# Short last chunks, small last groups and denominators by Ln and Exp in a two-part graph network kernel

## The chip, the core and the metric

The kernel runs on one core of a Trainium2 chip. Its time is the device time of one execution in microseconds (us); the time before is the median of 3 runs. The engines of the core work side by side, each through its own queue in order: PE (TensorE, matrix multiplies), DVE (VectorE), ACT (ScalarE), POOL (GpSimd, here nothing but indirect DMAs) and SP (the queue that issues the plain DMAs). They meet at semaphores.

## The reference

A graph of 10000 nodes with 64 features, and 160000 edges, sorted by their target dst. Part 0 has four layers (L = 4) of this convolution, between layer norms and residual sums:

```python
def _genconv(x, src, dst, ea, W1, b1, lg, lb, W2, b2, t):
    m = jax.nn.relu(x[src] + ea) + EPS
    logits = m * t
    mx = jax.ops.segment_max(logits, dst, num_segments=N)
    e = jnp.exp(logits - mx[dst])
    denom = jax.ops.segment_sum(e, dst, num_segments=N)
    alpha = e / denom[dst]
    agg = jax.ops.segment_sum(m * alpha, dst, num_segments=N)
    h = agg + x
    h = h @ W1 + b1
    h = jax.nn.relu(_ln(h, lg, lb))
    return h @ W2 + b2
```

Part 1 is one attention layer: K and V of the source node, Q of the target node and a projected edge feature give a score per head, `exp(clip(score, -5, 5))`; the output is the sum of V times score over the edges of a node, added to x.

## The kernel before, in words

**Stages.** An encoder over the nodes; index preparation; then for each layer l = 0 to 3 a loop over the edges (`softmax_layer(l)`) and a loop over the nodes (`node_layer(l)`); then a last edge loop (`attention_layer`), and a closing loop over the nodes that adds the residual and stores the output. After node layer 0, `clear_queries` sets the buffer `qs` in DRAM to zero with 157 DMAs on SP's queue; the scheduler puts 36 of them into the prologue and 121 between the stores of softmax layer 0 and the table rows of node layer 0.

**Edge loops.** The edges are worked from both ends at once: the first half forwards in partitions 0 to 63, the second half backwards in 64 to 127. There are NG = 625 groups of 128 edges for each half, taken in chunks of CG = 4 groups, so NC = 157 chunks: 156 of 512 columns and a last one of 128. For every group POOL issues two gathers (L603) of 128 rows of the node table, one for each half: 1250 for each edge loop. `front` adds them on PE to the transformed edge features (L687, L689), ACT makes the logits (L692, L693), and a scan on DVE (L699) gives the running maximum. `decay` writes the factor exp(-rise) into the PSUM tile `dec`, which has one buffer; `back` runs one chunk behind, with the product me (L727), the scans se (denominator, L729) and sm (numerator, L732), two transposes (L758), and four stores to the DRAM buffer st0 (L762). With the last chunk the node in the middle, which has edges in both halves, is corrected (L738 to L753). `attention_layer` is built the same way (scores L990 to L1002, back L1008 to L1025) with its store to st1.

**Order.** A scheduler places the instructions of the program on each engine. An object of the class `InOrder`, when called, ties all instructions since its last call, engine by engine, to the order in which the program makes them. It is called once for each chunk in the edge loops, but not after the last `back(NC - 1, *held)`; and once at the end of `node_layer`.

**Node layers.** NT = 79 tiles of 128 nodes, in groups of GRP = 8: ten groups, the last of 7. The stages of a group are spread over several turns i of a software pipeline:

```python
        for i in range(NG2 + (4 if last else 3)):
            at(i - 1, widen)
            at(i, enter)
            at(i - 3, norm_narrow)
            at(i + 1, divide)
            at(i + 2, fetch)
            at(i - 1, spans)
            at(i - 1, norm_wide)
            at(i - 2, narrow)
            if last:
                at(i - 4, project)
            at(i - 3, leave)
```

`fetch` gathers (POOL, L603) each node's numerators and denominators from st0 into n_g (two buffers). `divide` takes the reciprocal on DVE in place (L806) and multiplies into n_h (L807). `enter` transposes in pairs of node tiles and adds the old features (L813, n_hT). `widen` multiplies by W1 into the PSUM tiles pn and ept (L821) and squares on ACT (L825); `spans` averages the squares on PE; `norm_wide` takes Ln and Exp on ACT for the inverse root (n_r, L455 and L456), multiplies on DVE (n_y, L841, which frees pn and ept), and applies gain, bias and relu on ACT (L844). `narrow` multiplies by W2 (L851), adds into XT (L856) and squares (n_sx, L858). `norm_narrow` averages on PE (L863), Ln and Exp on ACT (n_rx), multiplies on DVE (XIT, L872; n_e in the last layer), and relu on ACT (L873). `leave` transposes back and stores the next layer's table rows (n_row L495, SP L487); the next edge loop's first gather needs them all. In the last layer `leave` forms the residual, and `project` makes K, V and Q (n_kvq, one buffer): K and V go to kv_table by SP, Q goes to `qs` by one scatter on POOL for each node tile (L906), each of which waits until the scatter before it has landed. A last scatter (mq, L1063) ends that, and then SP loads q from `qs`.

All tiles of a group are 512 columns wide, also for the last group of 7 tiles; what is missing there is filled by memset.

Of the kernel before, what the change touches and what calls it, by code (L numbers as in the profile page):

```python
# [9 lines left out]
F32 = mybir.dt.float32  # L10
# [3 lines left out]
OP = mybir.AluOpType  # L14
# [12 lines left out]
def kernel(ctx: ExitStack, tc: tile.TileContext, a, out):  # L27
# [21 lines left out]
    NG = HALF // G  # L49
    NC = (NG + CG - 1) // CG  # L50
    W = 1280
# [4 lines left out]
    MX = HALF - MR * MW  # L56
    assert 2 * NG * G == NE and R * W == NE and R <= P and NT <= P and MR < 64 and 0 < MX < MW
    EPS = 1e-7
    LN_EPS = 1e-5
    INV_SQRT_D = float(1.0 / (D // H) ** 0.5)  # L60
    GRP = 8
    groups = [(i, min(GRP, NT - i)) for i in range(0, NT, GRP)]

    const = ctx.enter_context(tc.tile_pool(name="const", bufs=1))
# [7 lines left out]
    def ps_a(shape):  # L72
        return ps("z", shape, 3)
# [377 lines left out]
    PN = GRP // 2  # L451

    def root(t, v):

        nc.scalar.activation(t, v, AF.Ln, bias=lneps)  # L455
        nc.scalar.activation(t, t, AF.Exp, scale=-0.5)  # L456

    def norm_rows(dst, src, n, name):

        mv = work.tile([P, GRP, 2], F32, name=name + "_mv", bufs=2)  # L460
        for i in range(n):
            st = work.tile([P, 6], F32, name=name + "_st", bufs=2)
            nc.vector.bn_stats(st, src[:, i, :])
            nc.vector.bn_aggr(mv[:, i, :], st)
        rs = work.tile([P, GRP], F32, name=name + "_rs", bufs=2)
        root(rs[:, :n], mv[:, :n, 1])
        for i in range(n):
            nc.vector.tensor_scalar(dst[:, i, :], src[:, i, :], mv[:, i, 0:1], rs[:, i:i + 1],
                                    op0=OP.subtract, op1=OP.mult)
        if n < GRP:  # L470
            nc.vector.memset(dst[:, n:, :], 0.0)

    def turn_pairs(rows):

        pt = ps_a([P, PN, P])
        for j in range(PN):
            nc.tensor.transpose(pt[:, j, :], rows[:, 2 * j:2 * j + 2, :].rearrange("p s d -> p (s d)"), ident)
        return pt.rearrange("p j n -> p (j n)")

    def turn_back(cols):  # L480
        pt = ps_a([P, PN, P])
        for j in range(PN):
            nc.tensor.transpose(pt[:, j, :], cols[:, j * P:(j + 1) * P], ident)
        return pt.rearrange("p j (s d) -> p (j s) d", s=2)
# [3 lines left out]

    def of_group(t, i0):
        return t[:, i0 * D:i0 * D + CN]  # L490

# [17 lines left out]
    for i0, n in groups:  # L509
        h = work.tile([P, GRP, D], F32, name="n_h", bufs=2)  # L510
        norm_rows(h, load_x(i0, n), n, "n_a")
        hT = work.tile([P, CN], F32, name="n_hT", bufs=2)
        nc.scalar.activation(hT, turn_pairs(h), AF.Relu)
        pt = ps("oe", [P, CN])
        nc.tensor.matmul(pt, encW, hT, start=True, stop=True)
        nc.scalar.activation(of_group(XIT, i0), pt, AF.Identity, bias=encb)
        to_message_table(tables[0], turn_back(of_group(XIT, i0)), i0, n)

# [87 lines left out]
    def span(k):  # L606
        g0 = k * CG
        n = min(CG, NG - g0)
        return g0, n, slice(g0 * G, (g0 + n) * G)
# [59 lines left out]
    def softmax_layer(l, ea_rows=None):  # L669
# [99 lines left out]
        for k in range(NC):  # L769
# [13 lines left out]
            order()  # L783
        back(NC - 1, *held)

    def node_layer(l):

        last = l + 1 == L
        NG2 = len(groups)
        it = [{} for _ in groups]  # L790
        halves = [slice(s * D, (s + 1) * D) for s in range(2)]
        order = InOrder()

        def fetch(g):
            i0, n = groups[g]
            t = edge.tile([P, GRP, D2], F32, name="n_g", tag="so", bufs=2)
            for i in range(n):
                gather(t[:, i, :], st0, ends[:, i0 + i:i0 + i + 1])
            if n < GRP:
                V.memset(t[:, n:, :], 1.0)  # L800
            it[g]["g"] = t

        def divide(g):
            t = it[g]["g"].rearrange("p n (h i c) -> p n h i c", h=2, i=2)
            h = work.tile([P, GRP, D], F32, name="n_h", bufs=2)
            V.reciprocal(t[:, :, :, 0, :], t[:, :, :, 0, :])  # L806
            V.tensor_mul(h.rearrange("p n (h c) -> p n h c", h=2), t[:, :, :, 1, :], t[:, :, :, 0, :])  # L807
            it[g]["h"] = h

        def enter(g):  # L810
            pt = turn_pairs(it[g]["h"])
            hT = work.tile([P, CN], F32, name="n_hT", bufs=2)
            V.scalar_tensor_tensor(hT, pt, EPS, of_group(XIT, groups[g][0]), op0=OP.add, op1=OP.add)  # L813
            it[g]["hT"] = hT

        def widen(g):
            hT = it[g]["hT"]
            it[g]["w"], it[g]["sq"] = [], []
            for s in range(2):
                pt = ps(("pn", "ept")[s], [P, CN])  # L820
                nc.tensor.matmul(pt, W1[halves[s], l, :], hT[halves[s], :], start=True, stop=True)  # L821
                it[g]["w"].append(pt)
            for s in range(2):
                sq = edge.tile([P, CN], F32, name="n_sq", tag="up")
                S.activation(sq, it[g]["w"][s], AF.Square, bias=b1[:, l:l + 1])  # L825
                it[g]["sq"].append(sq)

        def spans(g):
            it[g]["v"] = []
            for s in range(2):  # L830
                pv = ps(("dec", "hist")[s], [P, CN])
                nc.tensor.matmul(pv, over_all, it[g]["sq"][s], start=True, stop=True)
                it[g]["v"].append(pv)

        def norm_wide(g):
            it[g]["y"] = []
            for s in range(2):
                r = edge.tile([P, CN], F32, name="n_r", tag="e")
                root(r, it[g]["v"][s])
                y = work.tile([P, CN], F32, name="n_y", bufs=4)  # L840
                V.scalar_tensor_tensor(y, it[g]["w"][s], b1[:, l:l + 1], r, op0=OP.add, op1=OP.mult)  # L841
                it[g]["y"].append(y)
            for y in it[g]["y"]:
                S.activation(y, y, AF.Relu, bias=lnB[:, l:l + 1], scale=lnG[:, l:l + 1])  # L844

        def narrow(g):
            if last:
                it[g]["x"] = load_x(*groups[g])
            pt = ps("oe", [P, CN])
            for s in range(2):  # L850
                nc.tensor.matmul(pt[halves[s], :], W2[:, l, :], it[g]["y"][s], start=True, stop=True)  # L851
            x = of_group(XT, groups[g][0])
            if l == 0:
                V.tensor_scalar(x, pt, b2[:, l:l + 1], None, op0=OP.add)
            else:
                V.scalar_tensor_tensor(x, pt, b2[:, l:l + 1], x, op0=OP.add, op1=OP.add)  # L856
            sq = edge.tile([P, CN], F32, name="n_sx", tag="me", bufs=1)
            S.activation(sq, x, AF.Square)  # L858
            it[g]["sx"] = sq

        def norm_narrow(g):
            pt = ps_a([P, CN])
            nc.tensor.matmul(pt, over_half, it[g]["sx"], start=True, stop=True)  # L863
            r = edge.tile([P, CN], F32, name="n_rx", tag="lg", bufs=1)
            root(r, pt)
            i0 = groups[g][0]
            k = 0 if last else l + 1
            if last:
                h = work.tile([P, CN], F32, name="n_e", bufs=2)
            else:  # L870
                h = of_group(XIT, i0)
            V.tensor_mul(h, of_group(XT, i0), r)  # L872
            S.activation(h, h, AF.Relu, bias=normB[:, k:k + 1], scale=normG[:, k:k + 1])  # L873
            it[g]["e"] = h

        def leave(g):
            i0, n = groups[g]
            if not last:
                to_message_table(tables[l + 1], turn_back(it[g]["e"]), i0, n)
                return  # L880
# [3 lines left out]
            pt = ps_a([P, PN, P])  # L884
            for j in range(PN):
                nc.tensor.matmul(pt[:, j, :], it[g]["e"][:, j * P:(j + 1) * P], linW, start=True, stop=True)
# [3 lines left out]
        def project(g):  # L890

            i0, n = groups[g]
            h = edge.tile([P, GRP, D], F32, name="n_k", tag="u")
            norm_rows(h, XR[:, i0:i0 + n, :], n, "n_a")
            hT = edge.tile([P, CN], F32, name="n_kT", tag="u")
            S.activation(hT, turn_pairs(h), AF.Relu)
            kvq = work.tile([P, GRP, DQ], F32, name="n_kvq")
            for j in range(PN):
                pt = ps_a([P, 2, DQ])
# [41 lines left out]
    def attention_layer():  # L941
# [89 lines left out]
        for k in range(NC):  # L1031
# [10 lines left out]
            order()  # L1042
        back(NC - 1, *held)

    mq = const.tile([P, D], F32, name="mq")
# [21 lines left out]

    for i0, n in groups:
        g = work.tile([P, GRP, D], F32, name="n_h", bufs=2)
# [40 lines left out]
```

## Time and profile before

| | |
|---|---|
| time, median of 3 runs (lowest, highest) | 9191.0 us (9187.4, 9194.08) |
| profiled execution, its own time | 9191.01 us |
| its span, first to last instruction | 9189.2 us |
| mean granted TensorE clock | 0.638 |
| DMA: packets, bytes, mean rate | 2337156, 1000.33 MB, 109 GB/s |

The stages of the profiled execution, by the gathers and scatters of POOL (us from the start of the span; "pause" is POOL's idle time before the stage):

| stage | pause before | first | last ends | gathers |
|---|---|---|---|---|
| softmax 0 | 139.69 (after POOL's first work) | 141.65 | 1778.91 | 1250 |
| nodes 0 | 22.56 | 1801.47 | 1917.98 | 79 |
| softmax 1 | 53.85 | 1971.83 | 3565.72 | 1250 |
| nodes 1 | 22.37 | 3588.09 | 3690.91 | 79 |
| softmax 2 | 53.30 | 3744.21 | 5332.87 | 1250 |
| nodes 2 | 22.28 | 5355.15 | 5458.71 | 79 |
| softmax 3 | 53.25 | 5511.96 | 7100.12 | 1250 |
| nodes 3 (with 75 scatters) | 22.47 | 7122.59 | 7437.36 | 79 |
| attention (with 5 scatters) | 0.30 | 7437.66 | 9068.89 | 1250 |
| output | 15.06 | 9083.95 | 9182.37 | 79 |

How to read the profile: a line of the groups gives source line, engine, operation, output and input tiles, shapes and count; then the total busy time and the mean of one in ns; then the idle time of the engine before these instructions and what ended it. "issue" means that nothing the profile shows was waited for. Idle time of an engine costs something only where the end of the program waits for it.

### The profile page before, as it was taken

What the parts mean: (1) busy time and instruction counts of PE and PEld (TensorE: products, weight loads), DVE (VectorE), ACT (ScalarE), POOL (GpSimd) and SP (SyncE); (2) the same over time, 40 slices, a digit from 0 to 9 for tenths busy, and PEclk for the clock granted to TensorE, in tenths of its full rate; (3) what the DMA queues carried; (4) which work ended last, traced back from release to release, by engine and by line L of the source; (5) the groups of instructions that cost most, each with busy time, mean ns of one, the idle gap of its engine ahead of it and who ended that gap; (6) DMA issues with size and microseconds to landing.
All of it is one profiled execution on the core that took longest, in us unless ns stands there. A gap on an engine that the chain in (4) does not pass through costs nothing. (4 is left out here: it accounts for less than half of the span.)

```text
span 9189.2 us, 67135 instructions
## 1 busy us (share of the span) xinstructions
PE 4656.7 (51%) x16367; PEld 2863.3 (31%) x16367; DVE 5626.8 (61%) x7868; ACT 2966.5 (32%) x4794; POOL 6586.3 (72%) x6735
## 2 busy tenths in 40 slices
PE   5566566454444444544444454444444546666663
PEld 2343343322222222222222222222222234444442
DVE  6787777646566655566666655666666545555553
ACT  2444444343333333433333343333333311111110
POOL 3777777657777776577777757777776567777776
PEclk8766766665655556555555565555555678888886
DMA  4555555544444443344444424444444135555553
GB/s 126 125 125 125 125 126 126 161 151 103 104 102 105 102 104 85 75 105 102 105 103 104 104 65 95 104 103 105 102 104 99 51 91 128 127 127 126 126 127 83
DMA packets 2337156, 1000.33 MB, mean 109 GB/s; under 512 B 2017476, under 2 KB 2108873, under 8 KB 2336534
## 3 DMA queue, kind: packets, MB, share of 16 engines
q1 hardware_dynamic: 2121566, 723.83, 32.2%
q0 software_dynamic: 215200, 272.11, 13.6%
q8 instruction: 145, 2.38, 0.1%
q14 instruction: 245, 2.01, 0.1%
HBM read 523.94 MB, written 471.27 MB: 108 GB/s over the span
## 5 line engine op out<-in xcount | busy, mean ns | idle before, releaser
L603 POOL DMA_INDIRECT xg<-table,idxA x2500 | 2522.5, 1009 | 1060.9 <-issue 725.4
L603 POOL DMA_INDIRECT xg<-table,idxB x2500 | 2362.8, 945 | 761.9 <-issue 759.2
L689 PE MATMUL z<-ident,xg 128*128 128x128 f32 x5000 | 1490.6, 432 | 1427.0 <-DMA xg<-table,idxB 1426.7
L699 DVE TENSOR_TENSOR_SCAN u<-lg,u,pn 128x512 f32<-128x512 f32 x624 | 796.2, 1276 | 2205.7 <-ACT lg L693 2173.8
L689 PEld LDWEIGHTS z<-ident,xg 128*128 128x128 f32 x5000 | 1245.7, 311 | 2339.8 <-issue 1815.1
L687 PE MATMUL z<-ea,eencW 128*128 128x512 f32 (+1 forms) x1256 | 1201.6, 1059 | 403.2 <-ACT ea L636 400.5
L663 PE MATMUL pn<-ends_m,picks 104*128 104x512 bf16 (+1 forms) x628 | 346.1, 551 | 1470.1 <-DVE u L699 1467.3
L687 PEld LDWEIGHTS z<-ea,eencW 128*128 128x128 f32 x1256 | 363.7, 304 | 2122.2 <-issue 1487.4
L692 ACT ACTIVATE lg<-z 128x512 f32<-128x512 f32 (+1 forms) x628 | 373.6, 595 | 2008.5 <-PE z L689 2008.5
L704 ACT ACTIVATE up<-lg 128x512 f32<-128x512 f32 (+1 forms) x628 | 394.3, 628 | 1302.9 <-DVE lg L701 1302.9
L729 DVE TENSOR_TENSOR_SCAN se<-dec,se,e 128x512 f32<-128x512 f32 x624 | 791.5, 1268 | 0.0
L603 POOL DMA_INDIRECT kv<-kv_table,idxA x625 | 647.7, 1036 | 190.5 <-issue 144.2
L732 DVE TENSOR_TENSOR_SCAN sm<-dec,sm,me 128x512 f32<-128x512 f32 x624 | 781.5, 1252 | 0.0
L990 PE MATMUL z<-ident,kv 128*128 128x128 f32 x2500 | 480.7, 344 | 559.2 <-DMA kv<-kv_table,idxB 558.8
L603 POOL DMA_INDIRECT kv<-kv_table,idxB x625 | 596.3, 954 | 190.6 <-issue 182.0
L990 PEld LDWEIGHTS z<-ident,kv 128*128 128x128 f32 x2500 | 427.9, 245 | 674.9 <-issue 634.1
L714 ACT ACTIVATE dec<-up 128x512 f32<-128x512 f32 (+1 forms) x628 | 376.5, 600 | 661.4 <-DVE sm L732 657.2
L1002 ACT ACTIVATE sc<-sc 128x512 f32<-128x512 f32 (+1 forms) x157 | 98.6, 628 | 1484.7 <-DVE sc L1001 1484.7
L693 ACT ACTIVATE lg<-lg,teps,tcol 128x512 f32<-128x512 f32 (+1 forms) x628 | 508.9, 810 | 20.8
L603 POOL DMA_INDIRECT n_g<-st,ends x316 | 303.8, 961 | 208.1 <-issue 112.9
L701 DVE TENSOR_TENSOR lg<-lg,u 128x512 f32<-128x512 f32 (+1 forms) x628 | 437.6, 697 | 21.7
L758 DVE STREAM_TRANSPOSE so<-se 128x512 f32<-128x512 f32 (+1 forms) x628 | 428.6, 683 | 0.0
(253 smaller groups left out, 7232.9 us busy)
## 6 DMA issues: line engine op xcount, KB each, us to landing
st<-so SPq DMA_DIRECT2D x2496, 128.0 KB
ea<-eaT SPq DMA_DIRECT2D x624, 256.0 KB
xg<-table,idxA POOLq DMA_INDIRECT x2500, 2.4
xg<-table,idxB POOLq DMA_INDIRECT x2500, 2.5
qs<-zeros SPq DMA_DIRECT2D x156, 256.0 KB
er<-in_edge_attr_dram SPq DMA_DIRECT2D x312, 128.0 KB
eaT<-ea SPq DMA_DIRECT2D x156, 256.0 KB
q<-qs SPq DMA_DIRECT2D x156, 256.0 KB
```

Source lines behind the costliest of these rows:

```text
L603: nc.gpsimd.indirect_dma_start(out=t, out_offset=None, in_=table, in_offset=bass.IndirectOffsetOnAxis(ap=idx, axis=0))
L687: nc.tensor.matmul(z[:, :m], eencW, ea[:, :m], start=True, stop=False)
L689: nc.tensor.matmul(z[:, g * G:(g + 1) * G], xg[:, g, :, :].rearrange("p s d -> p (s d)"), ident, start=False, stop=(g == n - 1))
L693: S.activation(lg[:, :m], lg[:, :m], AF.Identity, bias=teps[:, l:l + 1], scale=tcol[:, l:l + 1])
L699: V.tensor_tensor_scan(u[:, 1:m + 1], lg[:, :m], pn[:, :m], last, op0=OP.max, op1=OP.add)
L701: V.tensor_sub(lg[:, :m], lg[:, :m], u[:, 0:m])
L704: S.activation(up[:, :m], lg[:, :m], AF.Relu)
L714: S.activation(dec[:, :m], up[:, :m], AF.Exp, scale=-1.0)
L729: V.tensor_tensor_scan(se[:, :m], dec[:, :m], e[:, :m], prev.get("e", zero1), op0=OP.mult, op1=OP.add)
L732: V.tensor_tensor_scan(sm[:, :m], dec[:, :m], me[:, :m], prev.get("m", zero1), op0=OP.mult, op1=OP.add)
L758: V.transpose(so[:, :m // 32, i, :], t[:, :m].rearrange("p (b e) -> p b e", e=32))
L990: nc.tensor.matmul(pt[:, g * G:(g + 1) * G], kvs[g // 2][:, g % 2].rearrange("p s d -> p (s d)")[:, d0::2], ident, start=True, stop=True)
```

## The change

It has four parts. The last five groups of an edge loop become chunks of 2, 2 and 1 instead of 4 and 1 (158 chunks instead of 157). Node layers and the output loop use the list `tapered`: eight groups of 8, then 6, 4, 2 and 3 (twelve instead of ten), and every operation on a group is as wide as its pairs of node tiles (`pairs(n) * P` columns); a memset is left only for an odd tile. The encoder keeps the old groups. The division takes Ln and then Exp with scale -1 on ACT in place of the reciprocal on DVE. Both kinds of edge loop call `order()` once more after the last `back`.

```diff
-    NC = (NG + CG - 1) // CG
+    chunks = [(g, CG) for g in range(0, NG - 5, CG)] + [(NG - 5, 2), (NG - 3, 2), (NG - 1, 1)]
+    NC = len(chunks)
...
     groups = [(i, min(GRP, NT - i)) for i in range(0, NT, GRP)]
+
+    sizes = [GRP] * ((NT - 15) // GRP) + [6, 4, 2, 3]
+    tapered = [(sum(sizes[:i]), n) for i, n in enumerate(sizes)]
...
+    def pairs(n):
+        return (n + 1) // 2
+
...
-        if n < GRP:
-            nc.vector.memset(dst[:, n:, :], 0.0)
-
-    def turn_pairs(rows):
+        if n % 2:
+            nc.vector.memset(dst[:, n, :], 0.0)
+
+    def turn_pairs(rows, n):
         pt = ps_a([P, PN, P])
-        for j in range(PN):
+        for j in range(pairs(n)):
             nc.tensor.transpose(pt[:, j, :], rows[:, 2 * j:2 * j + 2, :].rearrange("p s d -> p (s d)"), ident)
...
     def span(k):
-        g0 = k * CG
-        n = min(CG, NG - g0)
+        g0, n = chunks[k]
         return g0, n, slice(g0 * G, (g0 + n) * G)
...
         back(NC - 1, *held)
+        order()
...
-        NG2 = len(groups)
-        it = [{} for _ in groups]
+        NG2 = len(tapered)
+        it = [{} for _ in tapered]
...
+        def size(g):
+            i0, n = tapered[g]
+            return i0, n, pairs(n) * P
+
...
         def divide(g):
+            i0, n, c = size(g)
+            q = 2 * pairs(n)
             t = it[g]["g"].rearrange("p n (h i c) -> p n h i c", h=2, i=2)
             h = work.tile([P, GRP, D], F32, name="n_h", bufs=2)
-            V.reciprocal(t[:, :, :, 0, :], t[:, :, :, 0, :])
-            V.tensor_mul(h.rearrange("p n (h c) -> p n h c", h=2), t[:, :, :, 1, :], t[:, :, :, 0, :])
+            S.activation(t[:, :q, :, 0, :], t[:, :q, :, 0, :], AF.Ln)
+            S.activation(t[:, :q, :, 0, :], t[:, :q, :, 0, :], AF.Exp, scale=-1.0)
+            V.tensor_mul(h[:, :q, :].rearrange("p n (h c) -> p n h c", h=2), t[:, :q, :, 1, :], t[:, :q, :, 0, :])
             it[g]["h"] = h
...
         def widen(g):
+            i0, n, c = size(g)
...
-                nc.tensor.matmul(pt, W1[halves[s], l, :], hT[halves[s], :], start=True, stop=True)
+                nc.tensor.matmul(pt[:, :c], W1[halves[s], l, :], hT[halves[s], :c], start=True, stop=True)
...
-    for i0, n in groups:
+    for i0, n in tapered:
         g = work.tile([P, GRP, D], F32, name="n_h", bufs=2)
```

The other functions of the node layers (`enter`, `spans`, `norm_wide`, `narrow`, `norm_narrow`, `leave`, `project`) change in the same way as `widen`: each operand is cut to its first c columns, and loops over PN become loops over pairs(n).

## The prediction

> **What bounds the kernel now.** I read the page first, then the GpSimd queue (POOL) in order of time over all stages, then the tables by form, then the timelines of VectorE (DVE) and ScalarE (ACT) around the seams between stages. From the page:
>
> ```profile
> PE 4656.7 (51%) x16367; PEld 2863.3 (31%) x16367; DVE 5626.8 (61%) x7868; ACT 2966.5 (32%) x4794; POOL 6586.3 (72%) x6735
> POOL 3777777657777776577777757777776567777776
> ...
> L603 POOL DMA_INDIRECT xg<-table,idxA x2500 | 2522.5, 1009 | 1060.9 <-issue 725.4
> L603 POOL DMA_INDIRECT kv<-kv_table,idxA x625 | 647.7, 1036 | 190.5 <-issue 144.2
> ```
>
> A POOL at 72% does not look like a bound. But its idle time is 0.30 us after every gather ("issue"): a gather of 0.94 us comes each 1.25 us. Going through the POOL queue in time, I find no pause over 0.4 us inside any of the five edge loops (1250 gathers each). The long pauses are all at seams, for example in layer 1:
>
> ```profile
> 3564.78 0.94 POOL L603 DMA_INDIRECT xg<-table,idxB  x1 [0.30 <-issue]
> 3588.09 0.94 POOL L603 DMA_INDIRECT n_g<-st,ends  x1 [22.37 <-issue]
> ...
> 3689.55 1.36 POOL L603 DMA_INDIRECT n_g<-st,ends  x1 [0.30 <-issue]
> 3744.21 0.94 POOL L603 DMA_INDIRECT xg<-table,idxA  x1 [53.30 <-DMA ea<-eaT]
> ```
>
> The columns are start, length, engine, line, and the idle time before. So the time is: gathers, which the change does not touch, plus seams. The seams: 139.7 us of prologue; 22.4 to 22.6 after each of four softmax loops; 53.3 to 53.9 after node layers 0 to 2; 15.06 after the attention loop; in node layer 0 also a 16.51 stall; in node layer 3 a run of 79 scatters into qs that each wait for the one before.
>
> What costs what, and what decides the period of a node layer:
>
> ```profile
> L806 DVE RECIPROCAL n_g<-n_g 128x512 f32<-128x512 f32 x40 | 134.0, 3349 | 105.9 <-DMA n_g<-st,ends 105.7 <-issue 0.2
> L456 ACT ACTIVATE n_r<-n_r 128x512 f32<-128x512 f32 x80 | 50.4, 629 | 2.5
> L455 ACT ACTIVATE n_r<-dec,lneps 128x512 f32<-128x512 f32 x40 | 26.8, 671 | 36.8 <-PE dec L832 36.8
> L727 DVE SCALAR_TENSOR_TENSOR me<-z,e 128x512 f32<-128x512 f32 x624 | 425.9, 683 | 0.0
> L727 DVE SCALAR_TENSOR_TENSOR me<-z,e 128x128 f32<-128x128 f32 x4 | 1.2, 292 | 0.1
> ...
> 3701.10 0.69 DVE L872 TENSOR_TENSOR XIT<-XT,n_rx 128x512 f32<-128x512 f32 x1 [2.07 <-ACT n_rx L456]
> 3701.71 3.35 DVE L806 RECIPROCAL n_g<-n_g 128x512 f32<-128x512 f32 x1
> 3705.09 0.69 DVE L807 TENSOR_TENSOR n_h<-n_g 128x512 f32<-128x512 f32 x1
> 3705.70 0.74 DVE L841 SCALAR_TENSOR_TENSOR n_y<-pn,b,n_r 128x512 f32<-128x512 f32 x1
> ...
> 3716.21 0.75 DVE L841 SCALAR_TENSOR_TENSOR n_y<-pn,b,n_r 128x512 f32<-128x512 f32 x1 [2.12 <-ACT n_r L456]
> 3717.44 0.75 DVE L841 SCALAR_TENSOR_TENSOR n_y<-ept,b,n_r 128x512 f32<-128x512 f32 x1 [0.49 <-ACT n_r L456]
> ```
>
> Layer 1 repeats n_y (L841) at 3646.59, 3658.89, 3670.03, 3681.70, 3694.14, 3705.70: about 11.9 us a group, where the 8 gathers of a group need 10.0. So node layers are bound by a chain through DVE, PE and ACT, not by POOL. The reciprocal stands in that chain. In the last two rows it is gone (no group is left to divide), and n_y waits for ACT instead.
>
> [...] the trace has 629 (Exp) and 671 (Ln). [...] the trace has one table load in all (1283 ns), and the built kernel after has one too. [...] the trace has 3349 ns against 697 for a multiply of the same tile. [...] a quarter of the width costs 292/683 = 43% here.
>
> **The change part by part.**
>
> *Short last chunks, after each softmax loop.* The gathers stay where they are; their last five groups are worked off as 2, 2, 1 instead of 4, 1. Before: the last gather starts at 3564.78, DVE ends its last transpose at 3582.22, and eight stores (each some 0.49 us on SP's queue) follow from 3581.85 to 3585.88; 2.2 us later POOL goes on. They are eight because the scheduler put the big chunk's transposes behind the end correction; the new order() call keeps the order of the program, so its stores go earlier. After, with widths between the 128 and 512 rows (scan 0.48 and 1.28, so 0.75 at 256; others 0.42): the dec tile has one buffer, so ACT takes up a chunk only when the scan sm of two chunks earlier is over. Chain: sm of chunk 153 at 3562.2; u and lg of chunk 155 to 3565.2; back(154) 4.2 to 3569.3; u and lg of 156 to 3570.9; back(155) 2.3 to 3573.2; u and lg of 157 to 3574.5; back(156) 2.3 to 3576.8; the last scans 1.3; correction 2.0; two small transposes 0.46: 3580.6. Four small stores 1.7 and 2.2 to land: 3584.5 to 3585.4 against 3588.09. I take -3.1; bounds -1 (only the stores gain) and -5. Four times: **-12.4**.
>
> *After attention.* Same working: back of the last but one chunk is 1.6 instead of 2.6, and the wide exp before it is gone: DVE's end 9080.11 becomes 9077.1. **-3.0** (-1 to -4). The last output group adds 192 instead of 448 columns: **-0.35**.
>
> *Divide on ACT, period of a full group.* Before, from n_y to n_y: 0.68 until PE gets the pn bank, widening 2.36, transposes and over_half 2.54, Ln and Exp 1.35, XIT 0.70, then reciprocal 3.38 and multiply 0.61: 11.6 (seen 11.9). After: the reciprocal goes, but ACT runs in order: relu of XIT 0.76, Ln and Exp of the divide 1.24, Ln and Exp of n_r 1.33, and n_y waits for that, and the second n_y 1.23 more, so the ept bank comes later too. Sum 11.15; with the excess of 0.25 seen before, 11.4. So 3.35 us off DVE are worth about 0.5 a group: what is late next is ACT's n_r. Two early groups that wait for landed gathers gain 1.4 once.
>
> *Taper 6, 4, 2, 3 for 8, 7.* Twelve groups instead of ten, two more turns of the pipeline, in narrower tiles. Counting the same chain by widths from the n_y of group 7: turns of 9.7, 9.05, 6.45, 5.25, then 11.6 to the first gather of the next stage: 42.05, against 38.5 from that point before. In layer 1 that point comes at 3700.2 instead of 3705.70 (n_y of group 1 at 3632.9, 1.4 earlier than before; four turns of 11.4; then 11.15 and 10.6, as narrower groups enter), so the next stage starts at 3742.25 against 3744.21: -2.0. With turns of 11.15 it would be -3.5. I take -2.5; bounds +4 (fixed costs) and -7 (time shrinks with the width). Layers 1 and 2: **-5**. Layer 0: its table rows wait on SP's queue behind 121 qs<-zeros until 1898.97, DVE stalls to 1903.41, and what ACT gained earlier is lost there; -0.6 at the next turn, two turns more behind it: **+0.6** (-4 to +4).
>
> *Layer 3.* The first scatter comes 2.35 earlier. A group of eight scatters takes 20.4, and 2.38 between groups. Before, 75 of 79 scatters stand ahead of the first kv gather on POOL, the other four among the gathers at 1.29 each; after, 78 do, because the last group has 3. From the first scatter to the first kv gather: eight full groups 163.2, groups of 6, 4, 2 and the first two of 3 31.7, the five blocks of n_g gathers between them 30.3, five seams of 2.38, and one of 3.6 where two scatters don't cover the next group's work: 240.7 against 234.9. The first kv gather comes 5.9 - 2.35 = 3.5 later, and three scatters (3.9) less follow it: **-0.4** (+8 to -5). The q loads wait for the last scatter (mq); it now comes about 11 us after the first kv gather instead of 29, so no new wait.
>
> *At nothing:* in the encoder only the last group had a part width, still four pairs; gathers and their bytes are unchanged.
>
> Sum: -12.4 - 3.0 - 0.35 - 5 + 0.6 - 0.4 = -20.5. The profiled execution took 9191.01 (span 9189.2), which is the median (9191.0): **9170**.
>
> **The rivals.**
> 1. *Taper pays for itself only* (0.2): each layer's two more turns cost what I credit above, +4 in layers 0 to 2 and +4 in layer 3, tails as forecast: about 9187. For: a 128 wide operation still costs 43%. Against: POOL waits through the whole drain, so nothing else is lost.
> 2. *Drains shrink more* (0.15): stores at -4.5 each and nodes at -6: about 9148. For: handovers of some 0.04 us only. Against: the chain's fixed parts.
> 3. *Slower* (0.1): the divide's tile is strided (pieces of 32), and ACT now stands in the chain of every node group. If the pair costs 3.0 instead of 1.25 us, 1.75 more in the roughly 29 turns that the chain binds make +51: 9221. It decides from 2.0 us a pair (+20.5, no gain) and is measurably slower from 2.6. For: this access has no row on ACT before. Against: DVE's multiply of the same strides takes 697, no more than contiguous ones.
> 4. *It doesn't do what it says*: the built order shows Ln, Exp and the short chunks where the diff puts them; no chance kept.
>
> **How the numbers follow.** Forecast 0.55, own range 9158 to 9184. 0.2% is 18 us, about what a measurement tells here: faster means below 9173. The forecast lies on both sides of that, some 0.6 of it faster; with rival 2 that makes 0.5. Same: the rest of the forecast and nearly all of rival 1, 0.4. Slower 0.1. Range: 9148 to 9192.
>
> **What would show it.** POOL's pause after the softmax loops near 19.3, after attention near 12; n_y's period in layer 1 near 11.4; the pause before the next softmax loop, and the span from the first n_g to the first xg at 153.6 (156.1 before)[...]. A period under 10.5 or over 12.5, or pauses inside the edge loops, would make the prediction wrong.

## The result, and the profile after

Both kernels were timed in turn on one chip, 12 runs each: 9178.26 us median (9167.08 to 9188.23) after the change, 9186.02 us (9178.76 to 9195.38) before it. The ratio is 0.9991, 95% interval 0.9982 to 1.0: some 8 us less, no more than this measurement can tell from no change. The profiled execution of the changed kernel took 9179.64 us, its span 9177.8 us against 9189.2.

From the page of the changed kernel (busy time by engine, and POOL's busy tenths in 40 slices):

```profile
PE 4669.3 (51%) x16496; PEld 2870.7 (31%) x16496; DVE 5513.1 (60%) x7927; ACT 3042.5 (33%) x5019; POOL 6584.0 (72%) x6735
...
POOL 2777777657777776577777757777777557777776
```

DVE lost 114 us and ACT gained 76, and the span moved by 11.4: most of that work was not on the path. POOL's row is the old one in all but three of its 40 digits, because the gathers are the old ones. The seams, in POOL's queue in order of time (layer 1; start, length, engine, line, idle before):

```profile
3566.95 1.07 POOL L613 DMA_INDIRECT xg<-table,idxB  x1 [0.30 <-issue]
3586.57 0.94 POOL L613 DMA_INDIRECT n_g<-st,ends  x1 [18.55 <-issue]
...
3687.25 0.94 POOL L613 DMA_INDIRECT n_g<-st,ends  x1 [6.63 <-DVE n_h L824]
3698.75 0.94 POOL L613 DMA_INDIRECT n_g<-st,ends  x1 [9.31 <-DVE n_h L824]
...
3744.13 0.94 POOL L613 DMA_INDIRECT xg<-table,idxA  x1 [41.93 <-DMA table<-n_row]
```

The pause after the edge loop is 18.55 where it was 22.37. The pause before the next loop is 41.93 where it was 53.30, but that is no gain: the small groups now wait for n_h inside the node layer (6.63, 9.31), so its gathers end later. What counts is the stretch from the first n_g to the next xg. By stages of the two profiled executions, in us:

| stage | before | after | difference | predicted |
|---|---|---|---|---|
| prologue | 141.65 | 141.84 | +0.2 | 0 |
| pause after softmax 0 | 22.56 | 21.10 | -1.5 | -3.1 |
| pauses after softmax 1, 2, 3 | 22.37, 22.28, 22.47 | 18.55, 18.04, 18.27 | -12.3 | -9.3 |
| nodes 0, first n_g to next xg | 170.36 | 174.26 | +3.9 | +0.6 |
| nodes 1 | 156.12 | 157.56 | +1.4 | -2.5 |
| nodes 2 | 156.81 | 155.65 | -1.2 | -2.5 |
| nodes 3, to the first kv | 315.07 | 319.17 | +4.1 | +3.5 |
| softmax loops 0 to 3 | 6407.97 | 6410.84 | +2.9 | 0 |
| attention loop | 1631.23 | 1622.73 | -8.5 | -3.9 |
| pause after attention | 15.06 | 13.24 | -1.8 | -3.0 |
| output gathers | 98.42 | 100.39 | +2.0 | 0 |
| after the last gather | 6.83 | 6.16 | -0.7 | -0.35 |

The pauses gave what was forecast in sum; node layers 0 to 2 gave nothing and are 4.1 us longer together. Within the edge loops POOL pauses nowhere in either trace (its idle time before a gather is 0.30 to 0.32 us, and once 0.57, after the change); their differences are in the lengths of single gathers.

The n_y of the last groups of layer 1 in the changed kernel's DVE queue:

```profile
3687.66 0.75 DVE L862 SCALAR_TENSOR_TENSOR n_y<-pn,b,n_r 128x512 f32<-128x512 f32 x1 [0.68 <-ACT n_r L465]
3699.30 0.75 DVE L862 SCALAR_TENSOR_TENSOR n_y<-pn,b,n_r 128x512 f32<-128x512 f32 x1 [0.81 <-ACT n_r L465]
3709.34 0.62 DVE L862 SCALAR_TENSOR_TENSOR n_y<-pn,b,n_r 128x384 f32<-128x384 f32 x1 [0.59 <-ACT n_r L465]
3718.53 0.48 DVE L862 SCALAR_TENSOR_TENSOR n_y<-pn,b,n_r 128x256 f32<-128x256 f32 x1 [0.39 <-ACT n_r L465]
3725.74 0.35 DVE L862 SCALAR_TENSOR_TENSOR n_y<-pn,b,n_r 128x128 f32<-128x128 f32 x1 [1.37 <-ACT n_r L465]
3732.01 0.48 DVE L862 SCALAR_TENSOR_TENSOR n_y<-pn,b,n_r 128x256 f32<-128x256 f32 x1 [1.48 <-ACT n_r L465]
```

From group to group 11.6, 10.0, 9.2, 7.2, 6.3 us; every n_y waits for ACT's n_r. And what ACT does in one full turn:

```profile
3647.45 0.69 ACT L464 ACTIVATE n_rx<-z,lneps 128x512 f32<-128x512 f32 x1 [2.06 <-PE z L887]
3648.17 0.63 ACT L465 ACTIVATE n_rx<-n_rx 128x512 f32<-128x512 f32 x1
3649.55 0.81 ACT L896 ACTIVATE XIT<-XIT,normB,normG 128x512 f32<-128x512 f32 x1 [0.76 <-DVE XIT L895]
3650.27 0.62 ACT L822 ACTIVATE n_g<-n_g 128x512 f32<-128x512 f32 x1
3650.92 0.63 ACT L823 ACTIVATE n_g<-n_g 128x512 f32<-128x512 f32 x1
3651.46 0.67 ACT L464 ACTIVATE n_r<-dec,lneps 128x512 f32<-128x512 f32 x1
```

n_r, which the next n_y needs, stands behind two waits (2.06 and 0.76) for the n_rx chain of an older group, and behind Ln and Exp of a later one. The average in dec is not in the way: PE went on from it to hist at 3648.46. The two waits are not new, though: the kernel before has them too, with the same lengths. What did change in a turn shows when it is laid beside one of before (first before, then after):

```profile
3646.59 0.74 DVE L841 SCALAR_TENSOR_TENSOR n_y<-pn,b,n_r 128x512 f32<-128x512 f32 x1
3647.26 0.74 DVE L841 SCALAR_TENSOR_TENSOR n_y<-ept,b,n_r 128x512 f32<-128x512 f32 x1
...
3652.91 0.69 ACT L455 ACTIVATE n_rx<-z,lneps 128x512 f32<-128x512 f32 x1 [2.06 <-PE z L863]
...
3658.89 0.74 DVE L841 SCALAR_TENSOR_TENSOR n_y<-pn,b,n_r 128x512 f32<-128x512 f32 x1
```

```profile
3640.54 0.75 DVE L862 SCALAR_TENSOR_TENSOR n_y<-pn,b,n_r 128x512 f32<-128x512 f32 x1 [0.55 <-ACT n_r L465]
3641.78 0.75 DVE L862 SCALAR_TENSOR_TENSOR n_y<-ept,b,n_r 128x512 f32<-128x512 f32 x1 [0.49 <-ACT n_r L465]
...
3652.82 0.75 DVE L862 SCALAR_TENSOR_TENSOR n_y<-pn,b,n_r 128x512 f32<-128x512 f32 x1 [0.55 <-ACT n_r L465]
```

From n_rx to the next n_y it is 5.98 us before and 5.37 after (n_rx at 3647.45): 0.61 saved. But the second n_y, which frees the PSUM bank ept, comes 1.24 us after the first instead of 0.67. Before, both n_r were ready (the second at 3646.01) when the reciprocal and its multiply let DVE go on to n_y (3646.59), so the two n_y ran back to back; after, the second waits for ACT once more. PE fills ept next, and the transposes and the average of n_sx stand behind that, so n_rx starts 6.91 us after n_y instead of 6.32. The turn takes 12.28 us where it took 12.30: what ACT saved at one end is given back at the other.

One cost was not foreseen, in the output loop's gathers on POOL:

```profile
9168.21 0.94 POOL L613 DMA_INDIRECT n_h<-st,ends  x1 [1.95 <-DMA out_dram<-n_h]
```

n_h has two buffers, so the last group, of 3, takes over the buffer of the group of 4. The group of 2 between them is gathered in 2.5 us, and the store of the group of 4 has not landed by then.

### The profile page after: what moved, and what is told of

It is laid out like the page before. It is cut to its first block, busy times and chain, and to the rows that moved or that the text cites. A ratio compares the mean times of both kernels' runs of the same rounds, so it can differ in the third digit from the quotient of the medians.

```text
span 9177.8 us, 67981 instructions
## 1 busy us (share of the span) xinstructions
PE 4669.3 (51%) x16496; PEld 2870.7 (31%) x16496; DVE 5513.1 (60%) x7927; ACT 3042.5 (33%) x5019; POOL 6584.0 (72%) x6735
## 5 line engine op out<-in xcount | busy, mean ns | idle before, releaser
L708 DVE TENSOR_TENSOR_SCAN u<-lg,u,pn 128x512 f32<-128x512 f32 (+1 forms) x628 | 797.0, 1269 | 2197.7 <-ACT lg L702 2172.5
L738 DVE TENSOR_TENSOR_SCAN se<-dec,se,e 128x512 f32<-128x512 f32 (+1 forms) x628 | 791.6, 1261 | 0.0
L741 DVE TENSOR_TENSOR_SCAN sm<-dec,sm,me 128x512 f32<-128x512 f32 (+1 forms) x628 | 781.4, 1244 | 0.0
```

What stands on the lines that cost most here:

```text
L708: V.tensor_tensor_scan(u[:, 1:m + 1], lg[:, :m], pn[:, :m], last, op0=OP.max, op1=OP.add)
L738: V.tensor_tensor_scan(se[:, :m], dec[:, :m], e[:, :m], prev.get("e", zero1), op0=OP.mult, op1=OP.add)
L741: V.tensor_tensor_scan(sm[:, :m], dec[:, :m], me[:, :m], prev.get("m", zero1), op0=OP.mult, op1=OP.add)
```

## The experiments

The experiments ran on three chips, four kernels on each, and none of these chips was like the first: the kernel before took 10518.6, 10387.7 and 10383.2 us there. The waits of POOL for the kernel before on the third of them (total, times, longest) show two entries that are missing, or short, in the first trace:

```profile
POOL xg L603 <- remote: 622.8, 178, 13.1
...
POOL xg L603 <- PE z L689: 195.4, 47, 11.6
```

There the edge loops do pause for more than 1 us, 56 to 58 times in each of layers 1 to 3 and 204 to 206 us in sum, and the pause after a loop is about 60 us instead of 22. So whole times tell little of the first chip, and pauses alone mislead; what carries over is the stretch of a loop with its pause, what stands between the loop's last transpose and the next gather, and the turns of a node layer in which no gather is awaited.

**The order() call alone, and with the short chunks** (the kernel before with one or both):

```diff
         back(NC - 1, *held)
+        order()
```

> The kernel before with one part of the change only: order() once more after the last back of every edge loop; chunks, groups and division as before. Theory A (the short chunks make the gain, the order adds about a microsecond by letting the big chunk's four stores go before the end correction): the pause after softmax loops 1 to 3 goes from 22.3-22.5 us to 21-22, the pause after attention stays within 0.5 of 15.1. Theory B (the pause ended late because eight stores stood together behind the last transpose, so the order alone makes most of the gain): the pause falls to 19-20 us, and the short chunks are worth no more than 1-2 us beside it. Node layers as before in both (first n_g to next xg 156-157 us in layers 1 and 2). Time: A -2 to -5 us, B -10 us or more.

> The kernel before with the short last chunks (2, 2, 1) and the order() call, but with the old groups at full width and the reciprocal. Theory A (the seams add up, each part has its own): pauses after the softmax loops as in the changed kernel (18.0-18.6 us in layers 1 to 3, about 21 in layer 0), after attention 13.2, node layers 1 and 2 as before at 156-157 us; time about 15 us under the kernel before and so 3 to 6 us under the changed kernel. Theory B (part of the shorter pause comes from the node layer's first group, whose division waits for less): the pauses stay above 19.5 and the time is not under the changed kernel.

> The kernel before with only the order() call, a second time: the first four experiments fell on a chip where every kernel, the one before too, takes 14.5% longer (10518 us), with 55 pauses of POOL inside each edge loop that the other traces do not have. Where the loops run without pauses: Theory A (order about -1 us, short chunks about -3): pause after softmax loops 1 to 3 21-22 us against 22.3-22.5 before and 18.0-18.6 in the changed kernel, pause after attention 14.5-15.5. Theory B (order makes most of it): 19-20 us and 13-14.

Ratios to the kernel before: 0.9997 (0.9985 to 1.0009), 0.9996 (0.9982 to 1.0009) and, again the order alone, 0.9996 (0.999 to 1.0003). Pauses after softmax 1 to 3: order alone 57.1, 57.9, 57.0, with the short chunks 54.1, 54.3, 54.1 (same chip). But the loops with short chunks are about 3.6 us longer there, so that loop and pause together take 1822.0 and 1822.5 on the mean. Order alone on the second chip: 1817.3, against 1815.8, 1815.8 and 1816.3 for three kernels there that have the short chunks too. Where gathers are late, the short chunks are worth 1.5 us at most beside the order, and neither theory's numbers fit.

One part of the pause is alike on all four chips: the time from the end of DVE's last transpose of a loop to the first n_g. In layer 1 of before and then of the changed kernel the last transposes are these; the gathers that follow start at 3588.09 (a line of the prediction) and 3586.57 (shown above):

```profile
3581.96 0.26 DVE L758 STREAM_TRANSPOSE so<-sm 128x128 f32<-128x128 f32 x1
```

```profile
3582.29 0.27 DVE L767 STREAM_TRANSPOSE so<-sm 128x128 f32<-128x128 f32 x1
```

And with the order alone, x_order:

```profile
4206.62 0.27 DVE L758 STREAM_TRANSPOSE so<-sm 128x128 f32<-128x128 f32 x1
...
4210.85 0.94 POOL L603 DMA_INDIRECT n_g<-st,ends  x1 [57.12 <-issue]
```

In all four layers it is 5.6 to 5.9 us in both traces of the kernel before, 3.7 to 4.0 with the order alone on two chips, and 3.7 to 4.2 in the traces with the short chunks too. So the order() call by itself takes about 1.9 us off each of these stretches: four stores instead of eight follow the last transposes. The rest of the gain on the first chip lies before that, from the start of the last gather to DVE's end: 17.4 to 17.6 us before and 15.0 to 15.6 after in layers 1 to 3, but 17.7 and 18.0 in layer 0. If the parts add up, the short chunks are worth 2.1 us in layers 1 to 3 and nothing in layer 0; no run has one part alone on a chip like the first. Both theories were off: the order is about half.

**Both kernels themselves, on the third chip:**

> The kernel before itself, for its stages on the chip of this call. If that chip is like the last two (about 10400 us): both theories of the tail expect pauses after softmax loops 1 to 3 of more than the 57-60 us of the kernel with only the order() call; Theory A (order about 1 us, short chunks 3) 58-60, Theory B (order most of it) 60 or more, above all of the runs of order. Node layers 1 and 2: 170-173 us, as in the kernels with old groups. If the chip is like the first: as in the trace of before.

> The changed kernel itself, for its stages on the chip of this call. On a chip like the last two: pauses after softmax loops near 54 us; if Ln and Exp and the taper give nothing that counts in sum, node layers 1 and 2 are at 170-174 us like all four other combinations of groups and division; if the two together cost the 1 to 4 us that the first pair of traces seemed to show, they are above 174. Last turns of n_y: on the first chip 10.0, 9.2, 7.2, 6.3 us; with the reciprocal on the second chip 9.1, 8.3, 6.9, 6.3, so Ln and Exp should cost about 1 us in each of the wider of them.

After against before: 0.9998 (0.999 to 1.0007). Pauses 62.2, 59.7, 60.5 before and 54.7, 54.7, 55.0 after; loop and pause together 1819.0 and 1814.3 on the mean of layers 1 to 3, so 4.7 us a loop, about what the first chip shows (4.1 in the pauses). One loop makes much of that mean: the three differences are 8.6, 2.6 and 3.0.

Layers 1 and 2 took 179.0 and 178.2 us in after_2, against 170.0 and 172.4 in before_2. That profiled run (10400.55) lay 21 us over the median of its own kernel, and one turn of 16.2 us in it is out of line (ACT waits 5.98 us for PE there), so I rest nothing on this difference alone.

**Taper undone, and Ln with Exp undone** (each in the changed kernel):

```diff
-    sizes = [GRP] * ((NT - 15) // GRP) + [6, 4, 2, 3]
+    sizes = [n for _, n in groups]
```

```diff
-            S.activation(t[:, :q, :, 0, :], t[:, :q, :, 0, :], AF.Ln)
-            S.activation(t[:, :q, :, 0, :], t[:, :q, :, 0, :], AF.Exp, scale=-1.0)
+            V.reciprocal(t[:, :q, :, 0, :], t[:, :q, :, 0, :])
```

> The changed kernel with the old node groups (nine of 8, one of 7) in the node layers and the output loop; short chunks and Ln with Exp kept. Theory A (Ln and Exp gain only at the first groups of a layer, the period of a full group stays near 11.7 us, and the taper costs what its two more turns cost): layers 1 and 2 take 152-154 us from the first n_g to the next xg, against 157.6 and 155.7 in the changed kernel and 156.1 and 156.8 before; layer 3 to the first kv gather 313-315 against 319.2; the two pauses of 2 us in the output loop go; time 8 to 14 us under the changed kernel. Theory B (the taper does shorten the drain, and Ln and Exp lengthen the turns): layers 1 and 2 at 158 us or more, time at or above the changed kernel.

> The changed kernel with the reciprocal on DVE in place of Ln and Exp (at the true width of each group); short chunks and tapered groups kept. Theory A (Ln and Exp are worth 2 to 4 us a layer, all of it at the first groups): first n_g to next xg 159-162 us in layers 1 and 2, the mean of n_y's period over full groups within 0.3 of the 11.7 of both kernels, time 6 to 14 us over the changed kernel. Theory B (ACT's Ln and Exp in the chain of every group are what kept the node layers from gaining): 154-156 us in layers 1 and 2, time under the changed kernel.

> The changed kernel with the old node groups, a second time. Theory A (taper costs what its two turns cost): layers 1 and 2 152-154 us from the first n_g to the next xg against 157.6 and 155.7 in the changed kernel, layer 3 to the first kv gather 313-315 against 319.2, no pauses of 2 us in the output loop, sum of seams 8 to 14 us under the changed kernel. Theory B (the taper shortens the drain, Ln and Exp lengthen the turns): 158 us or more.

> The changed kernel with the reciprocal on DVE in place of Ln and Exp, a second time. Theory A (Ln and Exp worth 2 to 4 us a layer, all at the first groups): 159-162 us in layers 1 and 2, period of a full group within 0.3 of 11.7. Theory B (ACT's Ln and Exp in the chain kept the layers from gaining): 154-156 us. The first pair of runs on the slower chip, where the gathers of a node layer themselves take longer, gave 169.8 and 169.7 with the reciprocal and the taper, 172.5 and 169.0 with Ln, Exp and old groups: no more than 2 us apart, which speaks for neither.

Old groups: 0.9995 (0.9981 to 1.0009), then 0.9983 (0.9974 to 0.9992), the only one of these that is clear of no change; the changed kernel itself did not run on that chip. Reciprocal: 0.9995 (0.9983 to 1.0007), then 0.9996 (0.9988 to 1.0005). First n_g to next xg, layers 1 and 2, on the three slower chips:

| | reciprocal | Ln and Exp |
|---|---|---|
| old groups | 170.8, 172.2; 173.5, 172.3; 172.1, 170.6; 170.0, 172.4 | 172.5, 169.0; 173.0, 171.6 |
| tapered | 169.8, 169.7; 171.9, 172.0 | 179.0, 178.2 |

Neither change alone moves a layer. The pause in the output loop does go with the taper, as expected: its gathers take 98.31 us in both kernels with old groups, and 100.36 and 100.65 in the two with the taper and the reciprocal. The absolute values of my expectations were the first chip's; what they did decide is that undoing either one does not make the layers longer, which Theory A for the reciprocal had forecast (159 to 162 against 157.6). The turns tell why. Take the traces up to here, and the medians over the turns from group 1 to 7 in layers 1 and 2. With the reciprocal (seven traces) the second n_y comes 0.66 us after the first, and the next n_y 5.98 after n_rx, in every one; with Ln and Exp (four traces) it is 1.24 and 5.37 in every one. So the exchange of 0.61 for 0.58 comes with the division, on every chip and with either kind of groups. In layers 1 to 3 the first n_y comes 33.9 to 34.2 us after the first n_g with Ln and Exp and 35.5 to 36.4 with the reciprocal, in all these traces and the first two: some 1.9 us earlier. The last five turns of a tapered layer sum to 44.4, 42.4, 42.7 and 44.1 us with Ln and Exp (changed kernel, two chips, layers 1 and 2) and to 40.3, 39.4, 39.7 and 40.2 with the reciprocal (the two other chips): 3.5 us later. Most of that is the turn up to group 7, in which a group of 4 is divided: 11.1 to 11.6 us against 8.2 to 9.5. The groups by form show one reason, first of x_recip, then of the changed kernel (count, total, mean ns, idle before):

```profile
L822 DVE RECIPROCAL n_g<-n_g 128x512 f32<-128x512 f32 x32 | 107.1, 3348 | 95.1 <-DMA n_g<-st,ends 91.1 <-issue 3.9
L822 DVE RECIPROCAL n_g<-n_g 128x256 f32<-128x256 f32 x8 | 14.0, 1746 | 0.0
```

```profile
L822 ACT ACTIVATE n_g<-n_g 128x512 f32<-128x512 f32 x32 | 19.9, 622 | 146.5 <-DMA n_g<-st,ends 138.9 <-issue 7.6
...
L823 ACT ACTIVATE n_g<-n_g 128x256 f32<-128x256 f32 x8 | 3.3, 416 | 0.3
L822 ACT ACTIVATE n_g<-n_g 128x256 f32<-128x256 f32 x8 | 3.2, 400 | 0.0
```

A narrow tile takes 1.6 us off the reciprocal by itself, but only 0.43 off Ln and Exp together. So part of what the taper could save was DVE's reciprocal, which Ln and Exp had already taken away.

**Another order of a turn.** If ACT's queue is in the chain, its order is a lever. First try, on the changed kernel with old groups:

```diff
             at(i, enter)
-            at(i - 3, norm_narrow)
-            at(i + 1, divide)
-            at(i + 2, fetch)
             at(i - 1, spans)
             at(i - 1, norm_wide)
+            at(i + 1, divide)
+            at(i + 2, fetch)
+            at(i - 1, gain)
+            at(i - 3, norm_narrow)
             at(i - 2, narrow)
```

(`gain` is the relu of n_y, taken out of norm_wide.)

> The changed kernel with the old node groups and another order of a turn: the averages of the squares and norm_wide (n_r, n_y) go ahead of divide and norm_narrow on ACT, PE and DVE, and the relu of n_y after divide. If n_r was late because it stood behind Ln and Exp of n_g and of n_rx in ACT's queue (Theory A), n_y's period falls from 11.7 to about 10.2 us, where the 8 gathers of a group (10.0) bind, ACT is then busy about 9.7 us a turn, and layers 1 and 2 take 141-146 us; time 25 to 45 us under the changed kernel. If the period is set by ACT's and PE's whole work in a turn and not by its order (Theory B), it stays at 11.2 or more and layers 1 and 2 at 150 us or more.

Slower, 1.0022 (1.0013 to 1.003); n_y's period at the end of a layer rose to 13.1 to 13.6, layers 1 and 2 to 183.7 and 184.6. That is neither Theory A's 10.2 nor a period that stays, as in Theory B. PE's queue names what I had overlooked:

```profile
4240.16 1.11 PE L492 MATMUL z<-ident,XIT 128*128 128x128 f32 x4 [5.35 <-ACT XIT L899]
4241.20 1.22 PE L840 MATMUL pn<-n_hT,W 64*128 64x512 f32 x1
```

The transposes of leave, which need the relu of XIT, stand on PE ahead of the next group's W1 (L840). With norm_narrow late, PE idles 5.35 us. So leave has to come a turn later:

```diff
             at(i, enter)
+            at(i + 1, divide)
+            at(i + 2, fetch)
             at(i - 1, spans)
             at(i - 1, norm_wide)
+            at(i - 4, leave)
+            at(i - 3, norm_narrow)
+            at(i - 1, gain)
+            at(i - 3, gain_narrow)
             at(i - 2, narrow)
```

(The old places of divide, fetch, norm_narrow and leave are gone; gain_narrow is the relu of XIT.) The loop has NG2 + 4 turns in every layer. turn_recip keeps the reciprocal: there norm_narrow is ahead of norm_wide, and divide comes last.

> The changed kernel with the old node groups and a third order of a turn. In reorder PE stood at the transposes of leave, in front of the next group's W1, until n_rx, XIT and its relu were done, and n_y's period was 13.5 us. Here leave is a turn later; divide stands between the squares and n_r, where ACT waited for PE; n_rx after n_r; the relus last. ACT's work is 9.7 us a turn. Theory A (order of ACT's queue is what hid the gain of Ln and Exp): n_y's period near 10.0 on a chip where gathers come each 1.25 us (layers 1 and 2 at 141-148), near 11.3 where they come each 1.4 to 1.5 (160-166). Theory B (something else binds, such as PE at its lower clock): period 12 or more, no layer under 169 on such a chip.

> The same third order, with the reciprocal on DVE behind n_y and XT, out of the way of n_r, instead of Ln and Exp. ACT has 8.5 us of work a turn and DVE 8.3. Theory A (order, not the operation, decides): the same layers as turn_ln within 3 us, since both are then bound by the gathers. Theory B (ACT's load is what binds): faster than turn_ln by 1 us a turn, 5 to 8 us a layer.

turn_ln: 10337.38 us against 10383.15 before and 10379.41 for the changed kernel on the same chip, ratio to before 0.9959 (0.9945 to 0.9972). It beats both. ACT's queue in one of its turns at the end of layer 1:

```profile
4198.62 0.67 ACT L844 ACTIVATE n_sq<-ept,b 128x512 f32<-128x512 f32 x1
4199.19 0.62 ACT L822 ACTIVATE n_g<-n_g 128x512 f32<-128x512 f32 x1
4199.84 0.63 ACT L823 ACTIVATE n_g<-n_g 128x512 f32<-128x512 f32 x1
4200.37 0.67 ACT L464 ACTIVATE n_r<-dec,lneps 128x512 f32<-128x512 f32 x1
```

No wait is left here: Ln and Exp fill the time in which PE makes the averages. The turns are 8.7, 9.6, 9.2 and 9.0 us at the end of layer 1, where before_2 has 11.2, 11.6, 10.5 and 9.5; layers 1 and 2 take 162.0 and 169.5 us (in the second, one turn took 19.3, with 7.05 us in which ACT waits for a releaser that the trace does not name). Of the 41.7 us between the ends of the last gathers in turn_ln and before_2, node layers 0 to 2 give 22.4, loops with their pauses 14.0, and layer 3 5.1. Layer 1 fits Theory A and rules out B's "no layer under 169"; layer 2 misses A's 160 to 166. One rival is open: leave also came a turn later, and no kernel has exactly this order with the reciprocal, so how much of the gain is the order's and how much the cheaper division's is not shown.

turn_recip is slower, 1.005 (1.0036 to 1.0064), with turns of 14.7 to 16 us and a last one of 12.7. Its PE queue:

```profile
4260.44 1.09 PE L486 MATMUL z<-ident,n_h 128*128 128x128 f32 x4 [3.74 <-DVE n_h L823]
```

With divide last, the transposes of enter wait for the reciprocal's n_h, and the averages that n_r needs stand behind them. That is a fault of this place and no test of ACT's load: both theories' numbers were missed, and neither theory was tested by it.

## Why the prediction was right, and where its sum was not

9170 was forecast and 9178.3 measured, inside the range of 9148 to 9192. Luck had a part. The range reached past no change, so that lying inside it says little, and the kernel before came out at 9186.0 us in these runs, 5 under the 9191.0 from which the forecast started. Against it the change is worth 7.7 us in the medians and 11.4 in the profiles, where the sum said 20.5.

- *Tails: right in sum.* -12.4 forecast, -13.7 measured, from parts that missed both ways: 1.5 in layer 0 and 4.1 in each other layer, where 3.1 was forecast for all. In layer 1 the chain through dec and the scans ran as written: DVE's end 15.6 us after the start of the last gather (15.8 forecast), first n_g 19.6 (19.7 to 20.6 forecast). After attention -1.8 instead of -3.0, at the very end -0.7 instead of -0.35.
- *Price of Ln and Exp: right*, 622 and 629 ns (128x512, 32 of each), where the sum for a full group had 1.24 us for the pair, the author's estimate. In the trace of before the Exp of n_r (L456) has 629 ns at that size too. The slower rival needed 3.0 us a pair.
- *Period of a full group: the term that failed is the ept bank.* 11.9 to 11.4 forecast; from group 2 to 7 of layer 1 it is 11.82 before and 11.75 after. ACT's n_r is late next, as forecast, and the stretch from n_rx to n_y fell from 5.98 to 5.37, as its links say (5.38). The prediction also saw that the second n_y comes 1.23 after the first, "so the ept bank comes later too". But its links without that add up to 10.96, and a sum of 11.15 leaves 0.19 for it. Measured, the second n_y moved from 0.66 to 1.24 after the first, and PE's multiply into ept from 1.46 to 2.04. With 0.57 the same sum is 11.53, against 11.62 by its own sum for before: a gain of 0.09, where 0.07 was measured. By luck the first turns hid the error: group 7 came at 112.7 us after the first n_g, 112.1 forecast.
- *Drain of the taper: too short.* Forecast from group 7 on 9.7, 9.05, 6.45, 5.25 and 11.6 to the next xg, 42.05 in all; measured in layer 1 10.0, 9.2, 7.2, 6.3 and 12.1, in all 44.8, in layer 0 44.7 and in layer 2 42.6. With the reciprocal it is 42.3 to 44.2 in the four tapered layers 1 and 2, so Ln and Exp are not the main reason; the reason stays open. Layers 1 and 2 came to +0.3 instead of -5, layer 0 to +3.9 instead of +0.6. In layers 0 to 2 that is what rival 1 says (taper pays for itself only): +4 against 4.1 measured. Its +4 in layer 3 did not come, and its 9187 does not follow from its terms (9183 with +4 once for layers 0 to 2, 9191 with +4 for each).
- *Layer 3: right*, +4.1 to the first kv, 3.5 forecast; from the first scatter to the first kv 241.2 us, 240.7 forecast.
- *Output loop: missed*, 1.95 us for n_h's buffers.
- The attention loop gave 4.6 us more than the fewer scatters account for, the softmax loops 2.9 less; both without pauses, and not explained.

One part of the long chain is left open. The average of n_sx on PE (L887, two matmuls) takes 1.02 us in one turn of the changed kernel and 1.91 in the next; the granted clock is 1.00 and 0.50 there:

```profile
3634.00:3635.20 1.20, 1.20 (x6) 0.68 (x5) 0.69 (x1) 1.06 (x3) 0.94 (x1) 1.00 0.26 55
3645.40:3647.50 2.10, 2.10 (x5) 1.06 (x4) 0.69 (x1) 0.05 (x1) 1.74 (x2) 0.50 0.52 121
```

The columns are the window (us), its length, busy time by engine (PE, PEld, DVE, ACT, POOL), granted clock, DMA share and GB/s. Windows of two turns, of the changed kernel and then of turn_ln:

```profile
3639.00:3664.00 25.00, 19.99 (x44) 7.90 (x44) 9.80 (x15) 18.42 (x30) 19.20 (x20) 0.73 0.30 74
```

```profile
4183.00:4202.00 19.00, 15.06 (x49) 6.05 (x48) 10.15 (x17) 17.99 (x30) 7.04 (x7) 0.90 0.24 52
```

The same 30 instructions on ACT (18.4 and 18.0 us) take 25 or 19 us, with the clock at 0.73 or 0.90; in turn_ln ACT is busy for 18.0 of 19.0 us, so its own work is the limit there. Whether the lower clock is a cause of the longer turn or only goes with it was not tested, and the second window lies on another chip, later in its layer, where few gathers are left.

## What to carry to other kernels

Moving an operation to an idler engine pays only what the new queue does not give back. Follow the chain once around: here 0.61 us was saved between two links, and 0.58 lost because the same move made a PSUM bank free later. Read, on every engine in order, what stands ahead of the next link and which buffer it frees (two orders of a turn with the same operations gave ratios of 1.0022 and 0.9959 to the kernel before, on two chips). Two cures for the same microseconds, here a narrower tile (1.6 us off the reciprocal, 0.43 off Ln and Exp) and a cheaper operation, need not add up. When a pipeline is drained by smaller groups, look for every buffer that paced itself on the large ones (n_h's cost 1.95 us here).

## What the hardware showed that was not expected

The kernel before took 9186.0, 10518.6, 10387.7 and 10383.2 us on four chips, with a granted clock of 0.63 to 0.64 in the profiled runs on the first and the last. The same 1250 gathers of a softmax loop took 1594 us on the first and 1761 on the last (layer 1), with pauses that the trace puts down mostly to a releaser it does not name ("remote"); what is slower there stays open. A gain in a pause need not be a gain: on the second and the third chip the short chunks, beside the order, cut the pause by about 3 to 4 us and lengthened the loop by about 3.
